# Residual pair with low-rank adapters: half of G early, B0's products and E last, and W0's second identity on GpSimd

## The chip, the cores and the metric

The kernel runs on one core of a Trainium2 chip. Its engines are TensorE (PE in the profile, with its weight loads as PEld), VectorE (DVE), ScalarE (ACT), GpSimd (POOL) and SyncE (SP), which only issues transfers. The metric is the device time of one execution in microseconds. Before the change the median of three runs is 326.9 us (325.46 to 327.69).

## The reference

All is f32. `x` has shape (8, 256, 1024): eight batches of 256 tokens. Two layers with a residual each follow one another, and every batch picks its own adapters by an index:

```python
def layer0(x):   # R = 32, lora_A (5, 1024, 32), lora_B_w (1024, 32)
    base = jnp.einsum('bsi,oi->bso', x, W)
    low = jnp.einsum('bsi,bir->bsr', x, lora_A[labeler_index])
    return base + jnp.einsum('bsr,or->bso', low, lora_B_w) * 0.5

def layer1(x):   # R = 16, lora_As (32, 1024, 16), lora_Bs (32, 16, 1024)
    base_out = jnp.einsum('bti,oi->bto', x, W) + b
    lora_h = jnp.einsum('bti,bir->btr', x, lora_As[adapter_mapping])
    return base_out + jnp.einsum('btr,bro->bto', lora_h, lora_Bs[adapter_mapping]) * 2.0

x = x + layer0(x)
x = x + layer1(x)
```

Written as matrices, one batch is multiplied by (I + W0)ᵀ(I + W1)ᵀ, and small products of rank 32 and 16 are added to it.

## The kernel before

**Algebra.** The kernel first multiplies the two weight matrices, identities added, and afterwards sends all eight batches through that one 1024x1024 product M. Three small products carry the adapters through the weights: G, the eight adapters A of layer 1 times I + W0 (`prepare_down`, two halves h of 512 columns, kept in `gT`); B0, layer 0's shared factor, times I + W1 (`prepare_up`, two halves); and E, the product of B0 and A (`prepare_cross`). Large products are made from 512x512 or 256x256 blocks by a scheme of seven block multiplications in place of eight, so sums of blocks, made by VectorE, are operands of TensorE.

**Storage.** `w0n` holds W0 as eight slices k of 128 rows by 1024 columns. `load_w0(k, i)` (L173, transfer at L176) loads 512 of the columns of one slice. `diag_w0(k)` (L180, operation at L182) adds the identity to a slice: for k below 4 (`NB`) in the first 512 columns, from 4 up in the second. `w1T` holds W1 transposed. It comes as quarters `wq[h, i]` loaded to `units` by `load_w1` (L163, transfers at L168), each of four transfers with runs of 512 bytes, and turned by VectorE in `turn_w1` (L225: transposes at L227, the identity at L235, by VectorE for h = 0 and by GpSimd for h = 1). The first 256 rows of W1's first quarter come another way: as `w1_rows` (L945), turned by TensorE against an identity (L977) and copied out by VectorE and ScalarE (L1022, L1021), with the identity added at L1030.

**Order.** Every engine runs its instructions in the order in which the program writes them (`manual_schedule`). Transfers issued by SP and ScalarE share eight completion semaphores in turn, so a new transfer is issued only when the one that had the semaphore before has landed. SP issues, in this order: `w1_rows`, W0's slices 0 to 3 (first columns), the rest of W1's first quarter, W1's second quarter, W0's slices 4 to 7, B0, W1's third and fourth quarters, then W0's second columns (L1059) and x (L153). The adapters A are loaded by GpSimd (`load_a1`, L193) behind a one-element copy that waits for the first kept product (L195), and repacked by eight copies (L203).

**TensorE.** After a few warming matmuls and the transposes come 32 matmuls of the first product of four row groups (`first`, L1010 and L1012): 16 for the left 256 columns and 16 for the right. `keep_p1` (L294, ScalarE copy at L296) saves them. Two `Second` objects (L609; `one` and `other`) multiply the second product by the seven-part scheme, with `zero_inner` (L644), `z_sums` (L474), `Second.op.sums` (L416) and copies out by `keep` (L503, L505). Then come `prepare_up(0)`, `prepare_down(0)`, `prepare_up(1)`, `prepare_down(1)` and `prepare_cross()`, and then the main products (`mult`, L280, matmul at L282), the first of which is product 6 of `w_groups[0]` and needs the sums `sums_w1_first` (L354: L355 and L356) and `sums` (L260: L268, L269, L274, L275). While these run, VectorE turns the third and fourth quarters, forms M's first rows (`form`, L584, L601 to L607), adds W0's identities of slices 4 to 7 in the midst of `sums_w1_first` (L1072 to L1074), and makes the sums.

Of the kernel before, what the change touches and what calls it, by code (L numbers as in the profile page):

```python
# [10 lines left out]
ALU = mybir.AluOpType  # L11
# [9 lines left out]
P = 128  # L21
# [3 lines left out]
MLOW = 64  # L25
BIAS = 48
NWARM = 6
# [6 lines left out]
NQ = NH // 2  # L34
NB = 4
# [6 lines left out]
def kernel(  # L42
# [51 lines left out]
    ident = const.tile([P, P], F32, tag="ident", name="ident")  # L94
# [9 lines left out]
    m22 = const.tile([P, NB, NH], F32, tag="m22", name="m22")  # L104
# [54 lines left out]
    def new_w1(h: int, i: int):  # L159
        both = units[:, 4 * h + 2 * i : 4 * h + 2 * i + 2].rearrange("p u n -> p (u n)")  # L160
        return both.rearrange("p (t c) -> p t c", t=NR)

    def load_w1(wq, h: int, i: int, lo: int = 0, hi: int = NR):  # L163

        rows = slice(h * NH + lo * SQ, h * NH + hi * SQ)
        for g in range(NG):
            cols = slice(i * NH + g * P, i * NH + (g + 1) * P)
            nc.sync.dma_start(  # L168
                wq[g * SQ : (g + 1) * SQ, lo:hi, :],
                w1[rows, cols].rearrange("(t q) c -> q t c", q=SQ),  # L170
            )

    def load_w0(k: int, i: int):  # L173
        cols = slice(i * NH, (i + 1) * NH)
        rows = w0[(k // NB) * NH : (k // NB + 1) * NH, cols]
        nc.sync.dma_start(  # L176
            w0n[:, k, cols], rows.rearrange("(p m) c -> p m c", m=NB)[:, k % NB, :]
        )

    def diag_w0(k: int):  # L180
        diag = w0n[:, k].rearrange("p (i q m) -> p i m q", i=2, m=NB)[:, k // NB, k % NB]
        nc.vector.tensor_tensor(diag, diag, ident, ALU.add)  # L182

    def load_b0():
        nc.sync.dma_start(
            b0.rearrange("p (i m) r -> p i (m r)", i=2),
            lora_b0.rearrange("(i p m) r -> p i (m r)", i=2, m=NB),
        )
# [2 lines left out]
    a1_rows = work[:, 0 : 2 * NH].rearrange("p (b k r) -> p b k r", b=B, k=NK)  # L191

    def load_a1():  # L193

        nc.gpsimd.tensor_copy(a1_rows[0:1, 0, 0, 0:1], m22[0:1, 0, 0:1])  # L195
        for b in range(B):
            j = index(fixed1, b, N1, mybir.EngineType.Pool)
            nc.gpsimd.dma_start(
                a1_rows[:, b].rearrange("p (i m) r -> p i (m r)", m=NB),
                lora_a1[bass.ds(j, 1)].rearrange("o (i p m) r -> p (o i) (m r)", i=2, m=NB),  # L200
            )
        for b in range(B):
            nc.gpsimd.tensor_copy(a1[:, :, b, :], a1_rows[:, b])  # L203
# [45 lines left out]
    def new_bank():  # L249
        ring.append(ring.pop(0))  # L250
        return ring[-1]
# [382 lines left out]
    def load_inner(ps, tiles):  # L634

        p = m22[:, tiles, :].rearrange("p m (h n) -> p (m h) n", h=2)
        for i, part in ((2, 0), (4, 2), (5, 3)):
            nc.scalar.copy(slot(ps, i), p[:, part])
# [77 lines left out]
    def prepare_up(h: int):  # L716
        pm = new_bank()
        for k in range(NK):
            g = k % 4
            nc.tensor.matmul(  # L720
                pm[g * R0 : (g + 1) * R0, :],
                b0[:, k, :],
                w1T[:, k, h * NH : (h + 1) * NH],
                start=(k < 4),
                stop=(k >= NK - 4),
            )
        nc.scalar.copy(ups[1][:, h * NH : (h + 1) * NH], pm)
# [13 lines left out]

    gT = [work[:, (4 + h) * NH : (5 + h) * NH] for h in range(NO)]

    def prepare_down(h: int):
        pm = new_bank()
        for k in range(NK):
            nc.tensor.matmul(  # L747
                pm,
                a1[:, k].rearrange("p b r -> p (b r)"),
                w0n[:, k, h * NH : (h + 1) * NH],  # L750
                start=(k == 0),
                stop=(k == NK - 1),
            )
        nc.scalar.copy(gT[h], pm)
# [182 lines left out]
    with tc.manual_schedule(engines=ORDERED):  # L937
        make_identity(nc, ident)
        mid = NR // 2
        wq = {}  # L940
# [2 lines left out]
        w1_rows = units[:, 0].rearrange("p (t c) -> p t c", t=2)  # L943
        for t, engine in enumerate((nc.sync, nc.scalar)):
            engine.dma_start(w1_rows[:, t], w1[t * P : (t + 1) * P, 0:NH])  # L945
        for k in range(NB):
            load_w0(k, 0)
        load_w1(wq[0, 0], 0, 0, mid, NR)
        wq[0, 1] = new_w1(0, 1)
        load_w1(wq[0, 1], 0, 1)  # L950
        for k in range(NB, NK):
            load_w0(k, 0)
        load_b0()
        for i in range(2):
            wq[1, i] = new_w1(1, i)
            load_w1(wq[1, i], 1, i)
        nc.scalar.copy(s_all[:, 0:R0], ident[:, 0:R0])


        def warm_up(first, last):  # L960
            for n in range(first, last):
                bank, i = banks[6 + n // 4], n % 4
                nc.tensor.matmul(
                    bank[:, i * P : (i + 1) * P],
                    ident,
                    ident,
                    start=(i == 0),
                    stop=True,
                    skip_group_check=True,
                )  # L970

        warm_up(0, NWARM)
        w1_turned = [banks[4 + t].rearrange("p (m q) -> p m q", m=NB) for t in range(2)]
        for t in range(2):
            for m in range(NB):
                rows = w1_rows[:, t].rearrange("p (q m) -> p m q", m=NB)[:, m]
                nc.tensor.matmul(  # L977
                    w1_turned[t][:, m, :],
                    rows,
                    ident,  # L980
                    start=(m == 0),
                    stop=True,
                    is_transpose=True,
                    skip_group_check=True,
                )
        warm_up(4, 7)
        raw0, raw1 = load_indices(idx0, 0), load_indices(idx1, 1)
        nc.gpsimd.memset(scale, L1_SCALING)
        for half in range(2):
# [20 lines left out]
        def first(g, k: int, n: int):  # L1010
            cols = slice(n * NH // 2, (n + 1) * NH // 2)
            nc.tensor.matmul(  # L1012
                g.p1[:, cols],
                g.a[0][:, k, :],
                w1T[:, k, cols],
                start=False,
                stop=(k == NB - 1),
                skip_group_check=True,
            )

        nc.scalar.copy(w1T[:, 0:NB, P : 2 * P], w1_turned[1])  # L1021
        nc.vector.tensor_copy(w1T[:, 0:NB, 0:P], w1_turned[0])  # L1022
        for k in range(NB):
            diag_w0(k)
            if k == 0:

                part = w1T[0:MLOW, 0, 0:1]
                diag = bass.AP(part.tensor, part.offset, [part.ap[0], [D + 1, NB], [NB, MLOW]])
                same = ident[0:MLOW, 0:MLOW].unsqueeze(1).to_broadcast([MLOW, NB, MLOW])
                nc.vector.tensor_tensor(diag, diag, same, ALU.add)  # L1030
            for g in w_groups:
                first(g, k, 0)
        fixed0, fixed1 = fix_indices(raw0, N0, 0), fix_indices(raw1, N1, 1)
        for k in range(NB):
            turn_w1(wq[0, 0], 0, k, mid, NR)
        seconds = [Second(n) for n in range(2)]
        one, other = seconds
        zero_inner(one.ps)
        for m, g in enumerate(w_groups):
            for k in range(NB):  # L1040
                first(g, k, 1)
            g.keep_p1(m22[:, m, :])
            if m % 2:
                load_inner(seconds[m // 2].ps, seconds[m // 2].tiles)
        load_a1()
        for k in range(NB, NK):
            turn_w1(wq[0, 1], 0, k)
        one.products([1, 2])
# [11 lines left out]
            load_w0(k, 1)  # L1060
        other.products([6, 5, 4, 7, 3])
        keep(other.kept, other.ps)
        prepare_up(0)
        prepare_down(0)
        for k in range(NB):
            turn_w1(wq[1, 0], 1, k)
        one.form()
# [1 line left out]
            turn_w1(wq[1, 1], 1, NB + k)  # L1069
        for k in range(NB):  # L1070
            sums_w1_first(k)
            if k == 1:  # L1072
                for n in range(NB, NK):
                    diag_w0(n)  # L1074
        prepare_up(1)
        prepare_down(1)
        prepare_cross()
        w_groups[0].sums()
        sums_w1_last()
# [280 lines left out]
```

## Time and profile before

| what | value |
|---|---|
| median of three runs | 326.9 us |
| the profiled execution, whole | 325.97 us |
| its span in the profile | 323.9 us |
| granted TensorE clock | full throughout |
| matmul L1012, 32 of 128x256 in two passes | 7.05 to 21.5 us |
| products of `one` and `other` (L527) | 21.49 to 33.9 us |
| `prepare_up(0)`, `prepare_down(0)` | 33.93, 35.78 us |
| `prepare_up(1)`, `prepare_down(1)`, `prepare_cross` | 42.85, 45.38, 52.45 us |
| DMA queue of SP, software queue of GpSimd, whole span | 20.87 MB, 15.01 MB |

Starts are counted from the start of the span. The stretches of the profile below give busy microseconds of each engine with the number of its instructions behind it, then the granted clock, the share of the DMA engines' time, and GB/s.

```profile
core 0: us, PE busy (x) PEld busy (x) DVE busy (x) ACT busy (x) POOL busy (x), PEclk, DMA share, GB/s
0.00:7.00 7.00, 4.84 (x26) 4.54 (x26) 3.61 (x8) 2.09 (x3) 5.15 (x22) 1.00 0.68 230
7.00:21.50 14.50, 14.21 (x65) 12.56 (x66) 9.40 (x23) 2.65 (x6) 2.68 (x5) 1.00 1.18 208
21.50:36.00 14.50, 14.50 (x74) 11.14 (x73) 13.82 (x26) 5.23 (x13) 6.44 (x13) 1.00 1.20 179
36.00:53.00 17.00, 17.00 (x64) 6.61 (x63) 13.55 (x21) 2.12 (x4) 2.46 (x4) 1.00 0.65 172
53.00:115.00 62.00, 62.00 (x212) 39.61 (x208) 56.14 (x102) 14.34 (x30) 24.71 (x28) 1.00 0.70 125
115.00:324.00 209.00, 205.40 (x1062) 172.56 (x1060) 157.20 (x314) 33.43 (x71) 28.63 (x36) 1.00 0.37 89
```

Each f32 matmul of the program appears as two records. The share of DMA time can pass 1[...].

### The profile page before, as it was taken

The numbers are of one execution on the slowest core, as the hardware profiler recorded it, in microseconds if no ns is written. First come the engines' busy times: TensorE is split into PE (matmuls) and PEld (weight loads), VectorE is DVE, ScalarE is ACT, GpSimd is POOL, SyncE is SP. The second block draws the span as 40 slices with busy tenths as digits, with TensorE's granted clock in tenths as the row PEclk, the third lists the DMA queues.
The fourth block names the chain that finished last, engine by engine and source line by source line (L and its number), as shares of the span: only waits on it lengthen the run. The fifth ranks groups of instructions, "written<-read, shape, count | busy, mean of one in ns | idle before, by whom it ended". The sixth has DMA issues, their size and how long they took to land.

```text
span 323.9 us, 4417 instructions
## 1 busy us (share of the span) xinstructions
PE 317.9 (98%) x1494; PEld 247.0 (76%) x1494; DVE 253.7 (78%) x490; ACT 59.9 (18%) x125; POOL 70.1 (22%) x107
## 2 busy tenths in 40 slices
PE   7999999999999999999999999999999999999995
PEld 6888434444588878888878888878888878888884
DVE  5679599879999899999969686929775929632965
ACT  2052215000224223640010420000240000222000
POOL 6053232455132231671004000003100000000000
PEclk9999999999999999999999999999999999999999
DMA  7999954987264995796417610235630111100113
GB/s 223 188 227 171 267 127 78 170 139 152 56 100 85 193 165 95 112 172 108 129 68 187 153 34 0 92 104 146 156 74 0 65 67 65 65 2 0 66 67 130
DMA packets 64910, 36.42 MB, mean 112 GB/s; under 512 B 45508, under 2 KB 58932, under 8 KB 64888
## 3 DMA queue, kind: packets, MB, share of 16 engines
q1 hardware_dynamic: 56088, 20.87, 29.7%
q0 software_dynamic: 8656, 15.01, 22.5%
q8 instruction: 12, 0.20, 0.2%
q10 hardware_dynamic: 144, 0.26, 0.2%
q14 instruction: 10, 0.08, 0.1%
HBM read 19.02 MB, written 8.39 MB: 85 GB/s over the span
## 4 chain that ended last, share of the span: by engine, by line
PE 94%; DMA 3%; DVE 1%; issue 0%; SPq 0%; DVEq 0%
PE bank L527 71%; PE bank L282 11%; PE bank L797 4%; PE bank L747 4%; DMA units<-in_L_cond_W_dram 3%; PE bank L1012 2%; PE bank L720 1%; DVE w1T L227 1%; PE bank L815 1%; DVE w1T L235 0%; PE bank L761 0%; PE bank L547 0%; DVE work L885 0%; SPq L168 0%; DVEq L227 0%
## 5 line engine op out<-in xcount | busy, mean ns | idle before, releaser
L509 DVE TENSOR_TENSOR work<-bank,work 128x512 f32<-128x512 f32 (+1 forms) x56 | 32.1, 618 | 30.6 <-PE bank L527 15.4
L505 ACT COPY work<-bank 128x512 f32<-128x512 f32 (+1 forms) x60 | 27.6, 546 | 77.3 <-PE bank L527 52.2
L931 POOL DMA_DIRECT2D out_dram<-work x12 | 8.9, 743 | 115.8 <-DVE work L607 115.8
L240 DVE STREAM_TRANSPOSE units<-units 128x512 f32<-128x512 f32 x32 | 20.1, 680 | 6.8 <-DMA units<-in_x_dram 6.8
L527 PE MATMUL bank<-w0n,w1T 128*128 128x256 f32 x104 | 24.1, 379 | 0.0
L527 PE MATMUL bank<-w1T,s_all 128*128 128x256 f32 x88 | 22.3, 379 | 0.0
L527 PEld LDWEIGHTS bank<-w0n,w1T 128*128 128x128 f32 x104 | 19.8, 190 | 2.7
L527 PE MATMUL bank<-w0n,m 128*128 128x256 f32 x88 | 20.9, 380 | 0.0
L227 DVE STREAM_TRANSPOSE w1T<-units 128x512 f32<-128x512 f32 (+1 forms) x16 | 14.9, 984 | 6.9 <-DMA w0n<-in_L_cond_W_dram 3.7
L527 PEld LDWEIGHTS bank<-w0n,m 128*128 128x128 f32 x88 | 16.6, 190 | 2.6 <-issue 0.4
L527 PEld LDWEIGHTS bank<-w1T,s_all 128*128 128x128 f32 x88 | 16.7, 190 | 2.3
L527 PE MATMUL bank<-tw,m 128*128 128x256 f32 x68 | 16.8, 379 | 0.0
L527 PE MATMUL bank<-tw,s_all 128*128 128x256 f32 x64 | 16.1, 379 | 0.0
L805 ACT ACTIVATE a<-bank,shift,scale 128x256 f32<-128x256 f32 x4 | 2.3, 564 | 72.4 <-PE bank L797 72.4
L1012 PE MATMUL bank<-w1T,w0n 128*128 128x256 f32 x64 | 14.4, 382 | 0.9 <-DVE w1T L1030 0.7
L527 PE MATMUL bank<-m,units 128*128 128x256 f32 x64 | 15.1, 379 | 0.0
L797 PE MATMUL bank<-units,down 128*64 128x256 f32 x128 | 14.7, 382 | 0.0
L1012 PEld LDWEIGHTS bank<-w1T,w0n 128*128 128x128 f32 x64 | 12.4, 196 | 2.7 <-DVE w1T L1030 0.9
L527 PE MATMUL bank<-w0n,s_all 128*128 128x256 f32 x56 | 14.4, 379 | 0.0
L747 PE MATMUL bank<-w0n,a 128*128 128x512 f32 x32 | 14.3, 599 | 0.0
L527 PEld LDWEIGHTS bank<-tw,m 128*128 128x128 f32 x68 | 12.9, 190 | 1.8
L282 PE MATMUL bank<-tw,s_all 128*128 128x512 f32 x32 | 14.2, 595 | 0.0
(263 smaller groups left out, 662.1 us busy)
## 6 DMA issues: line engine op xcount, KB each, us to landing
units<-in_x_dram SPq DMA_DIRECT2D x128, 64.0 KB, 2.4
out_dram<-work POOLq DMA_DIRECT2D x12, 512.0 KB, 3.5
w0n<-in_L_cond_W_dram SPq DMA_DIRECT2D x16, 256.0 KB, 7.7
units<-in_L_cond_W_dram SPq DMA_DIRECT2D x13, 256.0 KB, 8.7
out_dram<-work SPq DMA_DIRECT2D x3, 512.0 KB, 2.8
down<-in_L_cond_lora_A_dram SPq DMA_DIRECT2D x32, 32.0 KB, 2.6
w1T<-m POOLq DMA_DIRECT2D x4, 256.0 KB, 5.3
s_all<-units POOLq DMA_DIRECT2D x2, 512.0 KB, 5.3
```

The costliest lines, as they stand in the source:

```text
L227: nc.vector.transpose(w1T[:, k, cols].rearrange("p (t q) -> p t q", q=SQ), wq[:, lo:hi].rearrange("p t (q m) -> p m t q", m=NB)[:, k % NB],)
L240: nc.vector.transpose(xT[:, NX * j : NX * (j + 1), :].rearrange("p c (t q) -> p c t q", q=SQ), xq[:, :, j, :].rearrange("p t (q c) -> p c ...
L282: nc.tensor.matmul(pm, a[:, k, :], b(k), start=first and k == 0, stop=(k == NB - 1), skip_group_check=not first,)
L505: nc.scalar.copy(at_home(v, n), whole(ps, n))
L509: nc.vector.tensor_tensor(at_home(v, n), whole(ps, n), at_home(v, n), ALU.add)
L527: nc.tensor.matmul(slot(ps, i) if dst is None else dst, lhs, rhs, start=BANK[i][0] not in started, stop=stop, skip_group_check=True,)
L720: nc.tensor.matmul(pm[g * R0 : (g + 1) * R0, :], b0[:, k, :], w1T[:, k, h * NH : (h + 1) * NH], start=(k < 4), stop=(k >= NK - 4),)
L747: nc.tensor.matmul(pm, a1[:, k].rearrange("p b r -> p (b r)"), w0n[:, k, h * NH : (h + 1) * NH], start=(k == 0), stop=(k == NK - 1),)
L797: nc.tensor.matmul(pl[n * MLOW : (n + 1) * MLOW, :], downs[n][:, k, :], x_b[f"{n + 1}{k // NB + 1}"][:, k % NB, :], start=(k == 0), stop=( ...
L815: nc.tensor.matmul(pl, join, low, start=True, stop=True, skip_group_check=True)
L931: eng.dma_start(out[b, :, h * NH : (h + 1) * NH].rearrange("(j p) d -> p j d", p=P), ob[:, 0:D].rearrange("p (j d) -> p j d", d=NH),)
L1012: nc.tensor.matmul(g.p1[:, cols], g.a[0][:, k, :], w1T[:, k, cols], start=False, stop=(k == NB - 1), skip_group_check=True,)
```

## The change

The change is confined to the first 53 us of the program.

- *Start.* W1's first rows are turned per slice m of four: two transposes into a bank of its own, a copy (VectorE for slice 0, ScalarE for 1 to 3), a 64x64 identity. Slice 3 is turned behind the first four products. Six warming matmuls remain of nine (18 records to 12). Of the four groups, those that don't need W0's identity of slice k are multiplied first.
- *SP's queue.* W0's slices 0 and 1, the rest of W1's first quarter, W0's slices 2 and 3; then, behind a one-element memset of VectorE, W0's slices 4 to 7, and only after them W1's second quarter, B0 and the rest.
- *A.* Six of its eight loads are issued by ScalarE, two by GpSimd, as soon as the indices are fixed. They stand in ScalarE's order ahead of `keep_p1`.
- *The second 16 products of L1012* go by slice for the first two slices of all groups, then by pairs of groups for the last two.
- *G.* Half 0 is multiplied right behind them, ahead of `one` and `other`; half 1 behind `other`; then `prepare_up(0)`, `prepare_up(1)` and `prepare_cross` together.
- *W0's second identity.* GpSimd adds it, ahead of its identities of W1's last quarter (L235) in its own order.

```diff
     def diag_w0(k: int):
...
-        nc.vector.tensor_tensor(diag, diag, ident, ALU.add)
+        engine = nc.vector if k < NB else nc.gpsimd
+        engine.tensor_tensor(diag, diag, ident, ALU.add)
...
     def load_a1():
-
-        nc.gpsimd.tensor_copy(a1_rows[0:1, 0, 0, 0:1], m22[0:1, 0, 0:1])
         for b in range(B):
-            j = index(fixed1, b, N1, mybir.EngineType.Pool)
-            nc.gpsimd.dma_start(
+            engine = nc.scalar if b < 6 else nc.gpsimd
+            j = index(fixed1, b, N1, engine.engine)
+            engine.dma_start(
...
-    def prepare_down(h: int):
-        pm = new_bank()
+    def prepare_down(h: int, pm):
...
-        for k in range(NB):
+        for k in range(2):
             load_w0(k, 0)
         load_w1(wq[0, 0], 0, 0, mid, NR)
-        wq[0, 1] = new_w1(0, 1)
-        load_w1(wq[0, 1], 0, 1)
-        for k in range(NB, NK):
+        for k in range(2, NB):
             load_w0(k, 0)
-        load_b0()
-        for i in range(2):
-            wq[1, i] = new_w1(1, i)
-            load_w1(wq[1, i], 1, i)
...
+        def turn_first(m: int):
+            for t in range(2):
                 nc.tensor.matmul(
+                    banks[4 + m][:, t * P : (t + 1) * P],
+                    w1_rows[:, t].rearrange("p (q m) -> p m q", m=NB)[:, m],
                     ident,
...
+            copy = nc.scalar.copy if m else nc.vector.tensor_copy
+            copy(w1T[:, m, 0:NQ], banks[4 + m][:, 0:NQ])
+
+        def diag_first(m: int):
+            diag = w1T[0:MLOW, m, 0:NQ].rearrange("p (q m) -> p m q", m=NB)[:, m]
+            nc.vector.tensor_tensor(diag, diag, ident[0:MLOW, 0:MLOW], ALU.add)
...
+        for m in range(2):
+            turn_first(m)
+            diag_first(m)
+            if m == 0:
+                diag_w0(0)
         for k in range(NB):
-            diag_w0(k)
...
+            if k + 2 < NB:
+                turn_first(k + 2)
+                diag_first(k + 2)
+            if k:
+                diag_w0(k)
+            if k == 1:
+                fixed1, fixed0 = fix_indices(raw1, N1, 1), fix_indices(raw0, N0, 0)
+
+                nc.vector.memset(w0n[0:1, NB:NK, 0:1], 0.0)
 
-            for g in w_groups:
+            for g in sorted(w_groups, key=lambda g: g.m % 2 == k % 2):
                 first(g, k, 0)
-        fixed0, fixed1 = fix_indices(raw0, N0, 0), fix_indices(raw1, N1, 1)
+        for k in range(NB, NK):
+            load_w0(k, 0)
+        load_a1()
+        wq[0, 1] = new_w1(0, 1)
+        load_w1(wq[0, 1], 0, 1)
+        load_b0()
+        for i in range(2):
+            wq[1, i] = new_w1(1, i)
+            load_w1(wq[1, i], 1, i)
...
-        for m, g in enumerate(w_groups):
-            for k in range(NB):
+        for k in range(NB // 2):
+            for g in w_groups:
                 first(g, k, 1)
-            g.keep_p1(m22[:, m, :])
-            if m % 2:
-                load_inner(seconds[m // 2].ps, seconds[m // 2].tiles)
-        load_a1()
+        for both in (slice(2, 4), slice(0, 2)):
+            for k in range(NB // 2, NB):
+                for g in w_groups[both]:
+                    first(g, k, 1)
+            for g in w_groups[both]:
+                g.keep_p1(m22[:, g.m, :])
+        for s in seconds:
+            load_inner(s.ps, s.tiles)
+        prepare_down(0, banks[3])
...
         keep(other.kept, other.ps)
-        prepare_up(0)
-        prepare_down(0)
+        for n in range(NB, NK):
+            diag_w0(n)
+        prepare_down(1, new_bank())
...
             sums_w1_first(k)
-            if k == 1:
-                for n in range(NB, NK):
-                    diag_w0(n)
+        prepare_up(0)
         prepare_up(1)
-        prepare_down(1)
         prepare_cross()
```

More of the change, by code (lines that the diff above doesn't have):

```diff
@@ L945 @@
             engine.dma_start(w1_rows[:, t], w1[t * P : (t + 1) * P, 0:NH])
-        for k in range(NB):
+        for k in range(2):
             load_w0(k, 0)
         load_w1(wq[0, 0], 0, 0, mid, NR)
-        wq[0, 1] = new_w1(0, 1)
-        load_w1(wq[0, 1], 0, 1)
-        for k in range(NB, NK):
+        for k in range(2, NB):
             load_w0(k, 0)
-        load_b0()
-        for i in range(2):
-            wq[1, i] = new_w1(1, i)
-            load_w1(wq[1, i], 1, i)
         nc.scalar.copy(s_all[:, 0:R0], ident[:, 0:R0])
-        def warm_up(first, last):
-            for n in range(first, last):
-                bank, i = banks[6 + n // 4], n % 4
+        for n in range(NWARM):
+            bank, i = banks[4 + n // 2], n % 2
+            nc.tensor.matmul(
+                bank[:, NQ + i * P : NQ + (i + 1) * P],
+                ident,
+                ident,
+                start=(i == 0),
+                stop=True,
+                skip_group_check=True,
+            )
+        def turn_first(m: int):
+            for t in range(2):
                 nc.tensor.matmul(
-                    bank[:, i * P : (i + 1) * P],
+                    banks[4 + m][:, t * P : (t + 1) * P],
+                    w1_rows[:, t].rearrange("p (q m) -> p m q", m=NB)[:, m],
                     ident,
[L966 to L981, printed above, removed]
+                    start=(m >= NWARM // 2 and t == 0),
                     stop=True,
@@ L985 @@
                 )
-        warm_up(4, 7)
+            copy = nc.scalar.copy if m else nc.vector.tensor_copy
[3 more added lines that the diff above has]
+            nc.vector.tensor_tensor(diag, diag, ident[0:MLOW, 0:MLOW], ALU.add)
         raw0, raw1 = load_indices(idx0, 0), load_indices(idx1, 1)
@@ L1019, in first @@
             )
-        nc.scalar.copy(w1T[:, 0:NB, P : 2 * P], w1_turned[1])
-        nc.vector.tensor_copy(w1T[:, 0:NB, 0:P], w1_turned[0])
-        for k in range(NB):
-            diag_w0(k)
[L1025 to L1030, printed above, removed]
-            for g in w_groups:
-                first(g, k, 0)
-        fixed0, fixed1 = fix_indices(raw0, N0, 0), fix_indices(raw1, N1, 1)
+        for m in range(2):
[3 more added lines that the diff above has]
+                diag_w0(0)
+        fixed0 = fixed1 = None
+        for k in range(NB):
+            if k + 2 < NB:
[7 more added lines that the diff above has]
+            for g in sorted(w_groups, key=lambda g: g.m % 2 == k % 2):
+                first(g, k, 0)
+        for k in range(NB, NK):
[7 more added lines that the diff above has]
+            load_w1(wq[1, i], 1, i)
         for k in range(NB):
```

## The prediction

> **What bounds the kernel now.** I read the page's engine shares first, then the chain of work that ended last, then TensorE's waits over the whole span, then the timeline of the first 54 us engine by engine.
>
> ```profile
> PE 317.9 (98%) x1494; PEld 247.0 (76%) x1494; DVE 253.7 (78%) x490; ACT 59.9 (18%) x125; POOL 70.1 (22%) x107
> ...
> PE bank L963 <- POOL ident masks.py:199: 1.5, 1, 1.5
> PE bank L1012 <- DVE w1T L1030: 0.7, 1, 0.7
> PE bank L1012 <- DVE w1T L235: 0.2, 1, 0.2
> ```
>
> TensorE waits three times, 2.4 us in all, and never after 15.77. In the chain in order of time it runs from there to 320.4. So whatever lets it enter that run earlier shortens the kernel by that much, and any new wait in the run lengthens it one for one. Nothing that only frees another engine counts. The lines that decide are these, of the timeline:
>
> ```profile
> 7.05 8.08 PEld L1012 LDWEIGHTS bank<-w1T,w0n 128*128 128x128 f32 x38 [0.89 <-DVE w1T L1030]
> ...
> 18.09 4.13 DVE L227 STREAM_TRANSPOSE w1T<-units 128x512 f32<-128x512 f32 x4 [1.77 <-DMA units<-in_L_cond_W_dram]
> ...
> 28.91 4.11 DVE L227 STREAM_TRANSPOSE w1T<-units 128x512 f32<-128x512 f32 x4
> ...
> 39.28 4.11 DVE L227 STREAM_TRANSPOSE w1T<-units 128x512 f32<-128x512 f32 x4 [3.73 <-DMA w0n<-in_L_cond_W_dram]
> ...
> 40.47 0.53 POOL L235 TENSOR_TENSOR w1T<-w1T,ident 128x128 f32<-128x128 f32 x1 [5.20 <-DVE w1T L227]
> ...
> 43.33 0.64 DVE L355 TENSOR_TENSOR tw<-w1T 128x512 f32<-128x512 f32 x1
> ...
> 46.15 1.26 DVE L182 TENSOR_TENSOR w0n<-w0n,ident 128x128 f32<-128x128 f32 x4
> ...
> 50.69 0.69 DVE L269 TENSOR_TENSOR s_all<-s_all,w0n 128x512 f32<-128x512 f32 x1
> ...
> 53.02 7.13 PE L282 MATMUL bank<-tw,s_all 128*128 128x512 f32 x16
> ```
>
> The reader is to see the last part. The first main product (L282, product 6 of group 0) needs sum 269 of VectorE, done at 51.38. TensorE comes to it at 53.02, so VectorE leads by 1.64 us. VectorE's only hole is the 3.73 us before the transposes of the last quarter of W1, whose last load landed at 39.1 (issued 24.2, 14.9 to landing). The DMA engines are full from 4 to about 40 us. One more number matters, of the issues of L176 in the window 39 to 39.5: the last slice of W0's second columns is issued at 39.1 and lands 6.7 us later, at **45.8**.
>
> **The change, part by part.** Everything is reckoned as the start of L282, 53.0 now, for three limits: TensorE's own work, VectorE's chain, GpSimd's queue. The latest decides.
>
> *Start.* Before, eight transposes and two 128x512 copies (0.69 and 0.59) go ahead of the 64x256 diagonal (0.65), and the first product starts at 7.05. After, two transposes do: rows land at 4.26, done 4.96; a 128x256 copy of VectorE, some 0.4 by the half of 0.69 plus overhead; a 64x64 diagonal, 0.27 by L235. First product at about 5.8, 1.25 earlier. VectorE then gets diagonal 3 (it waits for the transpose behind the first four products and ScalarE's copy, to about 8.5) ahead of W0's slice 1 (0.4), so products of slice 1 wait some 0.5 at 8.7. Two transposes between products cost 0.22, restarts 0.25. The 64 records of 0.216 (13.8) then end at 20.6, against 21.5 now: **0.9 earlier**. The new order of the second half removes the 0.24 wait; that is in the 20.6.
>
> *TensorE's work from there.* Before, 53.0 - 21.5 = 31.5 us, with a wait of 0.38 for bank zeroing and about 0.7 of L720 behind GpSimd's diagonals (2.61 against 1.92 for the first one). Without them 30.5. The five prepared products only change places: TensorE alone would reach L282 at 20.6 + 30.5 = **51.1**, 1.9 earlier. This is the whole gain to be had.
>
> *A's loads (`load_a1`).* G's half 0 now runs at 20.6, not 35.8. Its eight loads go from GpSimd at 18.4 to ScalarE (six) and GpSimd (two) at about 10.5, after the indices (9.75). ScalarE issues two of them only when an earlier W0 slice has landed (14 to 15); its copies L296 behind them are first needed near 18.5, so that is hidden. GpSimd's two took 8.3 to 10.8 to land: 19 to 21, plus a copy of 0.3 each. Cost 0 (cover: the second half of the products) to 1; I take 0.3, inside later slack.
>
> *SP's queue.* W0's slices 4 to 7 move ahead of W1's second quarter and, by the small memset, behind VectorE at about 10.2. By 9.4 the engines have moved 2 MB, which is all that is issued by then, so they run dry. Before, SP went on issuing from 5.3. From the first issue (0.90) to the first bytes took 1.1, so the lull is about 1.9. Of the 0.5 MB of A (the eight adapters of layer 1, `a`) in smaller packets I assume the same time as now. The last loads come from the engine that lags most, which has less of a lull: I take 0.7, ends 0 and 1.9. W1's second quarter needs the 4.5 MB that were in at 21.4 before (the landing of W0's slice 7), plus the lull, plus A's at some 2.3: **24.4**, against 18.0.
>
> *VectorE's chain.* From that landing to L269's end: 28.91 - 18.09 = 10.8; transposes 4.1; forming 2.6 (32.92 to 35.55); transposes 4.1; eight sums 5.45 (43.33 to 49.97, less the 1.26); two sums 1.4; in all 28.5. So 24.4 + 28.5 = **52.9**. Before, 18.0 + 28.5 + 3.7 of hole + 1.3 of L182 = 51.5, as seen. Moving G's product ahead has eaten the hole. On the way TensorE may stand 0.5 to 1 at the second products (bank zeroing L646 comes at 24.4 + 5.6, TensorE at 29.4); this is beside the later limit.
>
> *The second identity by GpSimd.* It takes 1.26 off VectorE, as four operations of some 0.53 (L235, the same shape). The row says VectorE's transposes took 4.11 beside L235 and 4.11 without it, but one sum (L356) took 0.90 beside it instead of 0.69. The Trainium skill, "Perfetto Trace Analysis", section "Optimizing Scalar/DVE Operations", says that GpSimd and VectorE share an SBUF read port, so that moving work between them might not help. By the rule, if every GpSimd operation blocked VectorE, 4 x 0.53 = 2.1 would come back and the step would cost 0.85 net, VectorE's chain being 55.0. By the row, beside transposes nothing comes back and 1.26 stays saved. I take the row, with 0.2 for one sum.
>
> What the step does to GpSimd's own queue is worse. In program order the four stand **ahead of L235**, the diagonals of W1's last quarter, and each waits for its slice of W0, the last at 45.8. VectorE's sums L355 wait for L235. So: last slice, +0.1, identity 0.53, +0.1, first L235 0.53, +0.05, then 6.85 to the end of L269 (5.45 + 1.4): landing + 8.15. With an unchanged landing, 45.8 + 8.15 = 53.95. With 0.7 of lull, 46.5 less 0.2 for A's loads that no longer fall between W1's: 46.3, so **54.45**. Ends: 43.0 (the slow engine catches up in the lull and A no longer goes through GpSimd's descriptors) gives 51.15; 48.5 (full lull, and x's loads squeezed in as now) gives 56.65. Meanwhile TensorE runs G's other half, waiting slice by slice, until about 47.8, then B0's two products and E, 4.5, and stands about 2 us at L282.
>
> *Others at nothing.* ACT's later copies, the loads of x and of A0 behind SP (x is turned from 98.8, A0 multiplied from 115.2) and the rearranged banks stay under the 35 us of L282. After L282 VectorE has lost its lead of 1.64, but 60 to 70 us shows it busy 6.51 of 10, so it gets this back.
>
> **Sum.** Start of L282 at 54.4 against 53.0: +1.4. Span 323.9 + 1.4 = 325.3; with the 2.07 around the span of the profiled execution (325.97) 327.4. The median shown, 326.9, is 0.9 above that execution, so **328.3**.
>
> **The rivals.**
> 1. *As meant.* The last slice lands by 43 and W1's quarter by 22.5; TensorE sets the pace: 51.1 to 51.7, 325.0 to 325.6. For it: A's loads ride in free time, and the slowest engine may use the lull. Against it: the same bytes must still pass a queue full until 40. 17%.
> 2. *VectorE's chain sets it* at 52.5 to 53.3: the slice is early but W1's quarter is late, 326.4 to 327.2. The change moves waits and gives nothing. 18%.
> 3. *The slower side: SP pinned behind the memset.* The DMA lull costs its full 1.9 or more and the last W0 slice lands after 48.2; there 8.15 more passes 56.35, 3.3 behind. At 49 the time is 331.0. For it: SP issued nothing less than full before. Against it: one engine lags the others by some us, so not all the lull is lost. 14%.
> Forecast (326.9 + 0.3 to 3.2: 327.2 to 330.1): 51%.
>
> **Numbers.** 1% is 3.3 us, about what a measurement of this kernel can tell from no change: 323.6 to 330.2. Faster than that isn't reached by rival 1 even whole (1.9 of gain); I leave 0.03 for an estimate of mine that is wrong. Slower: rival 3, 0.14, and a tail of the forecast, 0.15. Within: 0.82. The range leaves out the lower half of rival 1 and the upper half of rival 3: 325.3 to 330.7. The likeliest case alone is 327.2 to 330.1.
>
> **What would show it.** Right: TensorE waits for VectorE's sum L269 ahead of L282 for about 2 us; GpSimd's identities of W0 end with the last slice's landing, and L235 follows; L355 waits for GpSimd; first product near 5.8; hole in the DMA row at 10 to 11. Wrong: L282 starts before 52 with no wait (rival 1); the wait is there but L235 was done long before, with VectorE busy throughout (rival 2); A's copies end after 21.5 and TensorE stands ahead of G's half, which I hold to be hidden.

## The result, and the profile after

| | median, us | executions | ratio to before |
|---|---|---|---|
| before | 325.31 (324.3 to 327.69) | 22 | |
| after | 326.05 (325.02 to 328.03) | 22 | 1.003, 95% interval 1.0017 to 1.0044 |

The change costs about 1.0 us by this ratio (0.3% of 325.3; 0.55 to 1.4 by the interval); the means differ by 0.93, the medians by 0.74. The first three runs of the kernel before, of which the prediction took its level, lay high: their median 326.9 is 1.6 above that of all 22. The profiled execution of after took 327.88 us, its span 326.2; it is one of the longer ones, and the text below says where it is not typical.

TensorE's waits over the whole span of after (time in all, number, longest):

```profile
PE bank L282 <- DVE s_all L269: 2.0, 1, 2.0
PE bank L956 <- POOL ident masks.py:199: 1.5, 1, 1.5
PE bank L746 <- POOL a L203: 0.3, 1, 0.3
PE bank L967 <- DMA units<-in_L_cond_W_dram: 0.2, 1, 0.2
```

There is now a wait of 2.0 us ahead of the first main product. It was not there before. The timeline of after, with the lines that answer to those of before (line numbers have moved by a few; L1008 was L1012, L746 was L747):

```profile
6.22 3.78 PE L1008 MATMUL bank<-w1T,w0n 128*128 128x256 f32 x8
...
10.22 12.76 PE L1008 MATMUL bank<-w1T,w0n 128*128 128x256 f32 x56
...
23.27 7.13 PE L746 MATMUL bank<-w0n,a 128*128 128x512 f32 x16 [0.28 <-POOL a L203]
...
26.60 4.04 DVE L227 STREAM_TRANSPOSE w1T<-units 128x512 f32<-128x512 f32 x4 [9.29 <-DMA units<-in_L_cond_W_dram]
...
44.28 4.08 DVE L227 STREAM_TRANSPOSE w1T<-units 128x512 f32<-128x512 f32 x4
...
45.69 0.53 POOL L183 TENSOR_TENSOR w0n<-w0n,ident 128x128 f32<-128x128 f32 x1 [0.56 <-DMA w0n<-in_L_cond_W_dram]
46.16 1.01 POOL L235 TENSOR_TENSOR w1T<-w1T,ident 128x128 f32<-128x128 f32 x2
...
48.29 0.64 DVE L355 TENSOR_TENSOR tw<-w1T 128x512 f32<-128x512 f32 x1
...
54.48 0.69 DVE L269 TENSOR_TENSOR s_all<-s_all,w0n 128x512 f32<-128x512 f32 x1
...
55.32 1.95 PE L282 MATMUL bank<-tw,s_all 128*128 128x512 f32 x4 [1.96 <-DVE s_all L269]
```

VectorE's hole has moved. Before, there were 1.77 us ahead of W1's second quarter and 3.73 ahead of the last; now there are 9.29 ahead of the second quarter, and from 26.60 to the end of L269 at 55.17 VectorE works without a stop. GpSimd does let W1's identity (L235) stand behind the last slice of W0, but the first of them is done at 46.7, before VectorE has turned the quarter (48.36).

The DMA lull is where it was forecast. Stretches of before and then of after (busy time by engine, granted clock, share of DMA time, GB/s):

```profile
9.50:12.00 2.50, 2.50 (x13) 2.26 (x13) 1.11 (x8) 0.00 (x0) 0.00 (x0) 1.00 1.24 194
```

```profile
9.50:12.00 2.50, 2.50 (x10) 1.83 (x9) 1.02 (x7) 0.37 (x1) 0.00 (x0) 1.00 0.24 86
```

One thing in the timeline nobody asked for: the first eight records of L1008 take 3.78 us, 0.43 apart, where before they came 0.216 apart. In this execution TensorE ran at half speed until 10.8 us; the first record of the full clock is there, at 4.9 in the trace of before. (The clock's column says 1.00 in both rows above because it has no record earlier than that; the full clock given for the kernel before holds from 4.9 on.)

### The profile page after: what moved, and what is told of

It reads as the page before. It is cut to its first block, busy times and chain, and to the rows that moved or that the text cites. A ratio compares the mean times of both kernels' runs of the same rounds, so it can differ in the third digit from the quotient of the medians.

```text
span 326.2 us, 4400 instructions
## 1 busy us (share of the span) xinstructions
PE 318.7 (98%) x1488; PEld 248.3 (76%) x1488; DVE 252.2 (77%) x490; ACT 60.1 (18%) x127; POOL 67.0 (21%) x104
## 4 chain that ended last, share of the span: by engine, by line
PE 84%; DMA 10%; SPq 4%; DVE 1%; issue 0%; ACT 0%; ACTq 0%; DVEq 0%
PE bank L527 66%; PE bank L282 11%; DMA units<-in_L_cond_W_dram 6%; PE bank L796 4%; SPq L168 2%; DMA w0n<-in_L_cond_W_dram 2%; SPq L153 1%; PE bank L1008 1%; DMA work<-in_L_cond_lora_As_dram 1%; DMA down<-in_L_cond_lora_A_dram 1%; PE bank L967 1%; PE bank L814 1%; DVE s_all L269 0%; DVE s_all L268 0%; SPq L138 0%
## 5 line engine op out<-in xcount | busy, mean ns | idle before, releaser
L1008 PE MATMUL bank<-w1T,w0n 128*128 128x256 f32 x64 | 16.5, 420 | 0.0
L282 PE MATMUL bank<-tw,s_all 128*128 128x512 f32 x32 | 14.1, 594 | 2.0 <-DVE s_all L269 2.0
L1008 PEld LDWEIGHTS bank<-w1T,w0n 128*128 128x128 f32 x64 | 13.7, 219 | 2.4 <-DVE w1T L981 0.4
L746 PE MATMUL bank<-w0n,a 128*128 128x512 f32 x32 | 14.2, 595 | 0.3 <-POOL a L203 0.3
```

Of the source, the lines that this page charges most:

```text
L282: nc.tensor.matmul(pm, a[:, k, :], b(k), start=first and k == 0, stop=(k == NB - 1), skip_group_check=not first,)
L746: nc.tensor.matmul(pm, a1[:, k].rearrange("p b r -> p (b r)"), w0n[:, k, h * NH : (h + 1) * NH], start=(k == 0), stop=(k == NK - 1),)
L1008: nc.tensor.matmul(g.p1[:, cols], g.a[0][:, k, :], w1T[:, k, cols], start=False, stop=(k == NB - 1), skip_group_check=True,)
```

## The experiments

Three theories were tried. **G**, the prediction's: GpSimd's queue sets L282. **V**: VectorE's own chain from the landing of W1's second quarter does. **C**: the clock of TensorE turns a small wait into a larger loss.

### Eight warming matmuls (e1_warm8)

```diff
-NWARM = 6
+NWARM = 8
```

> The changed kernel with eight warming matmuls in place of six, so that TensorE stays busy until W1's first rows land. Theory C (clock): in the changed kernel's trace the full clock comes at 10.8 us instead of 4.9, because a short wait for the rows breaks the busy stretch; the longer warm-up brings it back to about 5 in nearly all executions: the group of executions near 327.4 thins out (9 of 22 now), median 325.3 to 325.6, ratio to before about 1.000 to 1.001. Rival (no clock effect, the two groups come from elsewhere): median stays 326.0 and the upper group stays at 4 of 10.

326.24 us, ratio 1.004 (1.0019 to 1.006): no gain. The profile has the full clock from 5.6, but the two extra matmuls run ahead of the transposes at half speed, the first product starts at 6.61, and L282 comes at 53.57 behind a wait of 2.2 us. Six of 22 executions had a mean granted clock of 0.995, at 327.8 to 329.2. A late start does not show in that mean (the execution traced for after has 0.998), so these six lost their clock later; where they did was not traced. The value of this run is as a trace of the changed order with an early clock.

### Before with six warming matmuls of nine (e2_before_short)

```diff
-        warm_up(4, 7)
```

> The kernel before with six warming matmuls in place of nine (the three behind the transposes left out). Theory C: TensorE then has nothing from 5.7 to 7.05 and more executions raise the clock late, so a second group some 2 us higher appears more often than before's 3 of 22, the ratio is 1.002 to 1.004. Rival: the three matmuls do nothing, ratio 1.000 and the groups as before.

325.69 us, ratio 1.0014 (0.9992 to 1.0036), inconclusive as a ratio; but five of 22 executions lie at 328.3 to 328.5, where the kernel before on the same chip had none of 51 above 327.6. The profile, of another execution (326.97), caught the clock's rise at 11.1 us, and its L282 came at 54.04, 1.0 later than in the profile of before. What makes the five longer by some 3 us was not traced. That leaving out the three matmuls makes a late clock more frequent is not shown: e12_before_ident below has all nine of them, and four of its 20 executions lie at 327.6 to 328.4. The changed kernel dropped the same three.

### GpSimd's two identities exchanged (e3_pool_order)

```diff
+            turn_w1(wq[1, 1], 1, NB + k)   # moved up: L235 now ahead
         for n in range(NB, NK):
             diag_w0(n)
         prepare_down(1, new_bank())
-            turn_w1(wq[1, 1], 1, NB + k)
```

> e1_warm8 with GpSimd's two kinds of identities in the other order: first W1's last quarter (L235), then W0's (L183); TensorE's order is unchanged. Theory G (the prediction's: L355 waits for L235, which waits behind the last slice of W0): L282 starts 1 to 1.5 us earlier than in e1_warm8, time 1 us less. Theory V (VectorE's own chain from the landing of W1's second quarter sets L282): no change, within 0.2 us of e1_warm8; TensorE may even lose 0.5 to 1 ahead of G's second half, since W0's identities come later.

329.64 us, ratio 1.0124 (1.0098 to 1.0151). L235 ran directly behind the transposes (first done at 43.5) and L269 still ended only at 53.72, against 53.42 in e1_warm8. This alone would not settle it, for the sums start 0.75 earlier here than there and then lose that beside W0's identities. The trace of e1_warm8 does:

```profile
40.13 0.90 DVE L604 TENSOR_TENSOR units<-units 128x512 f32<-128x512 f32 x1
...
43.72 0.52 POOL L235 TENSOR_TENSOR w1T<-w1T,ident 128x128 f32<-128x128 f32 x1 [0.49 <-DVE w1T L227]
...
46.52 0.66 DVE L355 TENSOR_TENSOR tw<-w1T 128x512 f32<-128x512 f32 x1
```

GpSimd, with W0's identities behind it, waits there for VectorE's transposes, and VectorE never for GpSimd. **Theory G falls.** In e3_pool_order TensorE instead waited for W0's identities, 3.7 us from 44.05. Timeline of this run, VectorE and GpSimd side by side, and then its stretches:

```profile
40.15 0.69 DVE L604 TENSOR_TENSOR units<-units 128x512 f32<-128x512 f32 x1
...
45.77 0.67 DVE L355 TENSOR_TENSOR tw<-w1T 128x512 f32<-128x512 f32 x1
...
46.77 3.73 POOL L183 TENSOR_TENSOR w0n<-w0n,ident 128x128 f32<-128x128 f32 x4
47.28 1.00 DVE L355 TENSOR_TENSOR tw<-w1T 128x512 f32<-128x512 f32 x1
```

```profile
40.00:47.30 7.30, 4.05 (x11) 1.71 (x9) 7.20 (x11) 1.84 (x4) 2.93 (x5) 1.00 0.59 135
47.30:50.70 3.40, 2.91 (x4) 1.35 (x5) 3.33 (x5) 0.00 (x0) 3.20 (x4) 0.50 0.31 61
50.70:54.00 3.30, 3.30 (x18) 1.10 (x20) 3.23 (x6) 0.59 (x1) 0.00 (x0) 1.00 0.20 32
```

Two more readings. The identity takes 0.93 (3.73 / 4) beside VectorE's sums, and a sum 1.00 in place of 0.67; in the changed kernel, beside forming and transposes, it took 0.55. And the second row shows the granted clock at 0.50: it fell 3.3 us into the wait, and stayed down for 3.4 us, 2.9 of them with TensorE back at work (from 47.79).

### Without the memset (e4_no_memset)

```diff
-                nc.vector.memset(w0n[0:1, NB:NK, 0:1], 0.0)
```

(on e1_warm8)

> e1_warm8 without the one-element memset, so that W0's slices 4 to 7 are issued as soon as a semaphore is free. Theory V: the lull of the DMA engines at 10 to 12 us goes, W1's second quarter lands 1.5 to 2 us earlier, VectorE's chain and L282 move by as much as TensorE allows: 1 to 1.5 us less than e1_warm8, below before by 0.3 to 1. Theory G: the last slice of W0 lands 0.7 earlier and so does L282. Rival: W0's slices 2 and 3 are slowed by the new traffic and TensorE waits for them at 8 to 10 us; no gain.

325.55 us, ratio 1.0001 (0.9984 to 1.0018); e1_warm8 stood at 1.004. The lull is gone (DMA share 1.06 from 9.5 to 12), W1's second quarter is turned from 22.1 instead of 24.7, the wait at L282 falls from 2.2 to 1.2, and none of 14 executions is at 0.995. The gain on e1_warm8, about 1.3 by the ratios, is of the size that theory V expected; the time did not fall below before. The landing came 2.5 earlier and L269 only 0.7 (52.74), since VectorE now stands 1.5 us ahead of its forming step, waiting for ScalarE's copies of the second product. As the run also brings W0's last slice earlier, it does not part V from G.

### Sixteen idle matmuls ahead of L282 (e5_fill)

```diff
         prepare_cross()
+        for n in range(16):
+            nc.tensor.matmul(
+                banks[7][:, P : 2 * P], ident, ident, start=True, stop=True, skip_group_check=True
+            )
```

> The changed kernel with 16 idle matmuls of the identity (some 1.8 us, into an unused part of a bank) between E and L282, where TensorE waits 2.0 us. Theory C2: in about a third of the executions that wait itself makes the clock fall to half for one stretch of 3.4 us, as it did in the trace of e3_pool_order; those are the executions with a mean clock of 0.995 (6 of 22 of the changed kernel, 327.0 to 328.0). The filler leaves no wait over 0.5, the executions at 0.995 go, and the median falls by 0.3 to 0.6 to about 325.6. Rival: the 0.995 has another cause, and its share stays, or the filler pushes L282 back and the time rises by up to 0.5.

328.15 us, ratio 1.0094 (1.0067 to 1.0121): a miss of mine. An idle matmul costs 0.23, not 0.11, since each makes two records, and the filler ran from 51.39 to 55.06, past the end of L269 at 52.51. As a trace it helps: it is the changed kernel with the clock early (its rise is at 5.1), and its sums are ready at 52.5, not at 55.2.

### W0's second identity back on VectorE (e6_ident_dve)

```diff
-        engine = nc.vector if k < NB else nc.gpsimd
-        engine.tensor_tensor(diag, diag, ident, ALU.add)
+        nc.vector.tensor_tensor(diag, diag, ident, ALU.add)
...
         one.form()
+        for n in range(NB, NK):
+            diag_w0(n)
+        prepare_down(1, new_bank())
```

> The changed kernel with W0's second identity back on VectorE, just ahead of the transposes of W1's last quarter. Theory V: VectorE's chain sets L282, so its four operations (1.26) come on top, more if they wait for the last slice of W0; L282 1.3 to 3 us later, time 1.3 to 3 more than the changed kernel, and more executions at 0.995 for the longer wait. Theory G: GpSimd's queue is free again, L235 directly behind the transposes, so 0.5 to 1.5 less.

329.06 us, ratio 1.01 (1.0072 to 1.0127), 3 more than the changed kernel: theory V again, and against G. L282 came at 53.67, behind a wait of 2.4 us (e5_fill's sums would have let it start near 52.7). That is about 1 us, under the 1.3 to 3 expected of the step; VectorE's chain itself grew by 0.7, from 28.5 (e5_fill) to 29.2. The rest is put down to the clock: 9 of 12 executions have a mean of 0.995 or less. The trace of one of them shows the wait (in this run L282 is line 281, and L269 line 268) and the fall at the place:

```profile
PE bank L281 <- DVE s_all L268: 2.4, 1, 2.4
```

```profile
50.00:53.90 3.90, 1.48 (x25) 0.74 (x18) 3.80 (x7) 2.32 (x5) 1.11 (x2) 1.00 0.22 36
53.90:57.30 3.40, 3.40 (x5) 1.39 (x5) 3.40 (x7) 1.34 (x3) 1.40 (x2) 0.51 1.04 151
57.30:60.00 2.70, 2.70 (x7) 1.14 (x6) 2.70 (x6) 0.60 (x2) 2.46 (x3) 0.99 0.79 146
```

TensorE is back at work at 53.67, and from 53.9 to 57.3 it works all the time at half clock: 1.7 us lost after the wait is over.

### No memset, and B0's load last (e7_no_memset_b0)

```diff
-                nc.vector.memset(w0n[0:1, NB:NK, 0:1], 0.0)
...
-        load_b0()
         for i in range(2):
             wq[1, i] = new_w1(1, i)
             load_w1(wq[1, i], 1, i)
+        load_b0()
```

> The changed kernel without the memset, and with B0's load behind W1's last quarter. Theory V with the last loads: without the lull W1's last quarter lands about 41 and, B0 (128 KB) being behind it, at about 41; L282 near 52, wait under 0.7, no executions at 0.995; 325.0 to 325.4, at or below before. Rival: TensorE's late clock at the start, still there in some executions, keeps the median at 325.5 or more.

325.22 us, ratio 0.9993 (0.9976 to 1.0009): level with before. The wait at L282 is 0.8; one of 22 executions is at 0.995. VectorE stands 1.6 us ahead of its forming step, as it did in e4_no_memset, so the last load no longer sets its chain.

### All of A's loads by GpSimd (e8_a_pool)

```diff
-            engine = nc.scalar if b < 6 else nc.gpsimd
+            engine = nc.gpsimd
```

> The changed kernel with all of A's loads issued by GpSimd. They no longer take turns with SP's loads on the eight shared semaphores, so W1's second quarter is issued and lands 1 to 2 us earlier (Theory V: L282 1 us earlier) if the semaphores held it back. But A lands later: the eighth issue comes 7 us behind the first, at about 19, and needs 5 or more to land, so TensorE waits ahead of G's first half by 2 to 4 us, which costs as much as it is not absorbed by the wait at L282: 0 to 2 slower than the changed kernel. If the semaphores are no matter, W1's second quarter lands as now.

332.56 us, ratio 1.0221 (1.0189 to 1.0253). TensorE waits 6.9 us for A ahead of G's first half (20.71 to 27.62), more than I had reckoned, and the clock falls 5.2 us into the wait, for 6.8 us. W1's second quarter is turned from 24.4, about as in e5_fill (24.0): there is no sign that the shared semaphores hold it back.

### Six idle matmuls (e9_fill6)

```diff
+        for n in range(6):
+            nc.tensor.matmul(
+                banks[7][:, P : 2 * P], ident, ident, start=True, stop=True, skip_group_check=True
+            )
         prepare_cross()
```

> The changed kernel with six idle matmuls of the identity ahead of E: e5_fill showed that one costs 0.22, so 1.3 us, less than the wait at L282 (1.8 to 2.0). Theory C2: the executions with a mean clock of 0.995 (6 of 22 of the changed kernel) go, for the wait left is 0.5 to 0.7; median 325.5 to 325.8, 0.3 to 0.5 below the changed kernel's 326.05. Rival: the 0.995 stays at a quarter, median 326.0 or above.

325.27 us, ratio 1.0001 (0.9987 to 1.0015), and none of 14 executions at 0.995. Idle work inside the wait, which can do nothing but keep TensorE busy, takes away the loss: **theory C holds for the wait at L282**. TensorE's waits in the profile (of one of the longest executions, 326.51):

```profile
PE bank L746 <- POOL a L203: 1.1, 1, 1.1
PE bank L282 <- DVE s_all L269: 0.2, 1, 0.2
```

### G's first half back behind the second product (e11_g_late)

```diff
-        prepare_down(0, banks[3])
...
+        prepare_down(0, new_bank())
         prepare_down(1, new_bank())
```

> The changed kernel with G's first half back behind the second product, all else as changed. Theory V: TensorE ends L1012 near 20.8 and W1's second quarter, now behind W0's slices 4 to 7 and A, lands at 24 to 26.5 and is turned by 28 to 30.5, so TensorE waits some 5 to 7 us for it, VectorE's chain stays as it is and L282 goes to about 58: 4 to 6 us slower than the changed kernel, with the clock falling on top. That would show that G's first half pays for its own loads only, by covering them. Rival: W1's second quarter lands earlier without G's early use of the engines, no more than 2 slower.

330.69 us, ratio 1.0151 (1.0118 to 1.0184). TensorE waits 5.2 us ahead of the second product (from 21.50), and the clock falls 3.3 us into the wait, for 6.8 us; L282 comes at 59.42 with no wait. In the new order of loads G's first half is needed as a cover.

### The identity alone, in the kernel before (e12_before_ident)

```diff
-        nc.vector.tensor_tensor(diag, diag, ident, ALU.add)
+        engine = nc.vector if k < NB else nc.gpsimd
+        engine.tensor_tensor(diag, diag, ident, ALU.add)
```

> The kernel before with W0's second identity by GpSimd alone (at its old place, behind L235). TensorE came to L282 1.64 us behind VectorE there, so 1.26 taken from VectorE brings nothing: ratio 0.999 to 1.001. If VectorE's later work mattered it would be below 0.998; if GpSimd's operations slow VectorE's sums by the shared port, VectorE's lead shrinks but the time stays.

325.49 us, ratio 1.0019 (0.9999 to 1.0038): no gain, as expected, though a little above the expected 0.999 to 1.001. Four of 20 executions lie at 327.6 to 328.4, at full mean clock; they were not traced. The four identities took 3.77 us in a row beside the sums.

### Two sums moved ahead (e10_sums_early)

```diff
         one.form()
+        w_groups[0].sums_first()
         for k in range(NB):
             turn_w1(wq[1, 1], 1, NB + k)
...
-        w_groups[0].sums()
+        w_groups[0].sums_last()
```

(on e7_no_memset_b0)

> e7_no_memset_b0 with the first two sums of W0's blocks (L268 and L269, 1.4 us) ahead of the transposes of W1's last quarter, in the hole of 2 us where VectorE waits for its load. Theory V: VectorE's chain after that load shortens by 1.4, starts at most 0.6 later, L282 comes some 0.8 earlier and the wait of 0.78 goes: 324.5 to 324.8, faster than before by 0.2%. Rival: TensorE is late by itself (late clock at the start, A's copies), time as e7_no_memset_b0, 325.2.

**324.07 us, ratio 0.9969 (0.9951 to 0.9986): faster than both kernels**, by 1.0 us against before. Its timeline, VectorE and then TensorE:

```profile
40.66 1.01 DVE L268 TENSOR_TENSOR s_all<-w0n 128x512 f32<-128x512 f32 x1
41.70 0.69 DVE L269 TENSOR_TENSOR s_all<-s_all,w0n 128x512 f32<-128x512 f32 x1
42.31 4.06 DVE L227 STREAM_TRANSPOSE w1T<-units 128x512 f32<-128x512 f32 x4
...
46.98 0.91 DVE L356 TENSOR_TENSOR tw<-tw,w1T 128x512 f32<-128x512 f32 x1
...
51.18 0.69 DVE L356 TENSOR_TENSOR tw<-tw,w1T 128x512 f32<-128x512 f32 x1
```

```profile
50.24 0.62 PE L760 MATMUL bank<-a,b 128*32 128x128 f32 x16
50.79 1.55 PE L282 MATMUL bank<-tw,s_all 128*128 128x512 f32 x3
```

The gain is larger than expected, for another reason than the hole I had named. VectorE did not sit idle there; the sums stand in its way like any other work. But L282's four matmuls need the sums of W0 whole and W1's sums one after the other: with L269 early, the first matmul needs only the first L356 (47.9), and the last L356 is done at 51.87, while the fourth matmul's turn comes 2.6 us after 50.79. TensorE has no wait left there, and L282 starts at 50.8, 0.3 from the 51.1 that the prediction gave for TensorE alone.

## Why the prediction was right and where it was wrong

**Right.** The direction and the kind of loss: a gain at the start, and a new wait of some 2 us at L282 for VectorE's sum L269. The first product was put at 5.8 and came at 5.9 to 6.0 in the traces of e5_fill and e9_fill6. G's first half was put at 20.6 and came at 20.8 in e5_fill, 0.7 before the point that before had reached at 21.5; with the late clock of after the gain at the start is lost. TensorE's own work from there was put at 30.5 and took 30.0 in e10_sums_early (the 0.38 that the prediction took out as a wait is idle time of the weight load, PEld). The lull lies where it was said. W1's second quarter was put at 24.4; it is turned from 24.0 (e5_fill), 24.7 (e1_warm8) and 24.9 (e9_fill6). VectorE's chain from there was put at 28.5 us and measured 28.6 (26.60 to 55.17). A's loads, held to be hidden, made TensorE wait 0.3 us in after and 1.1 in e9_fill6, inside the slack at L282.

**Wrong: the step that named the limit.** The prediction said that GpSimd's queue was the latest of three, "landing + 8.15", with the last slice of W0 at 46.3 and L282 at 54.45. In the traces of e1_warm8, e5_fill and e9_fill6 that slice lands at 42.3 to 43.1, 3 to 4 us before the estimate and at the low end that the prediction gave (43.0); with 8.15 on top, GpSimd's queue would let L269 end at 50.5 to 51.3. Even in the trace of after (45.7) L235 was done ahead of VectorE's need. The limit was rival 2's, VectorE's chain, put at 52.9 and found at 52.5 to 53.8 for an early clock. The error was to take the landing of 45.8 over from before and add a lull: in these three traces SP issued the slice at 36.3 to 37.0, where before had 39.1, and it then took about 6 us to land, where before took 6.7. The engine that lags is there in the trace of before (the trace keeps the landing of each of a transfer's 16 parts: of that slice the last lands 2.2 us behind the fifteenth) and hardly in these (0.5 at most). What let SP issue earlier is not shown.

**Wrong: the sum has no term for the clock.** The prediction let a new wait lengthen the kernel "one for one". With the limit where it was, L282 moved little: the changed kernel with an early clock has its sums ready at 52.5 to 53.8, where L282 stood at 53.0 in the profile of before. With the wait filled (e9_fill6) the ratio is 1.0001, so the loss hangs on the wait, and in part on what the clock makes of it. The table has the wait at L282 in each profile (for e3_pool_order that at G's second half, for e8_a_pool at its first, for e11_g_late at the second product), and the executions whose mean clock was 0.995 or less. That mean is what one stretch of 3.4 us at half clock makes of some 325 us. Such a stretch was traced in e3_pool_order and at L282 in e6_ident_dve; for the other kernels' executions at 0.995 the place is inferred.

| kernel | wait, us | executions at 0.995 or below |
|---|---|---|
| before, beside the experiments | 0 | 0 of 133 |
| e10_sums_early | 0 | 1 of 20 |
| e9_fill6 | 0.2 | 0 of 14 |
| e7_no_memset_b0 | 0.8 | 1 of 22 |
| e4_no_memset | 1.2 | 0 of 14 |
| after | 2.0 | 6 of 22 |
| e1_warm8 | 2.2 | 6 of 22 |
| e6_ident_dve | 2.4 | 9 of 12 |
| e3_pool_order | 3.7 | 6 of 6 |
| e11_g_late | 5.2 | 5 of 5 |
| e8_a_pool | 6.9 | 6 of 6 |

A stretch of 3.4 us at half clock costs 1.7 us if TensorE works through it; six of 22 would give 0.46 in the mean. As measured, those six of after (327.4 in the mean; the other sixteen 326.0) make 0.4 of the 0.93. The other half is not located: in e1_warm8 and e9_fill6 L282 comes at 53.6 and 53.9, up to 0.9 later than before, and three more executions of after lie at 327.3 to 327.9. That the forecast's +1.4 lies near the measured +1.0 is luck: a limit that was not the limit, and no clock.

**Wrong in level.** 328.3 stood on a median of three runs that was 1.6 too high.

**Left open.** The trace of after itself is of another kind: half clock at the start until 10.8, 2 us late from there on. How many of the changed kernel's executions are of this kind is not known (the three at 327.3 to 327.9 have a mean clock of 0.998 or 1.0, and one of them is the traced one), nor is its cause. The single executions at 0.995 of kernels with little or no wait were not traced.

**The rule on the shared port.** The prediction weighed the warning of the Trainium skill ("Perfetto Trace Analysis", section "Optimizing Scalar/DVE Operations") against GpSimd beside VectorE, and took the row of the trace. For transposes the row held: four took 4.08 beside identities and 4.04 without (44.28 and 26.60 in after). For sums both sides were slowed, as the rule warns: 0.93 for an identity, 1.00 for a sum (e3_pool_order). And in the changed kernel the identities fall not only on the last transposes but on forming, which is made of sums: the five forming steps take 3.0 to 3.3 us in after, e1_warm8, e5_fill and e9_fill6, and 2.5 in e3_pool_order and e6_ident_dve, where no identity of GpSimd runs beside them. So 0.5 to 0.8 of the 1.26 that VectorE was freed of came back, where the prediction had put 0.2, and 2.1 for the rule taken whole.

## What to carry to other kernels

When a product is moved ahead to cover late loads, follow the engine that prepares the operands behind those loads: its hole, not its busy share, says how much delay it can take. Price a new wait of a busy TensorE with the clock in it: here, by their mean clock, about a quarter of the executions paid some 1.5 us on top of a wait of two, and cheap idle matmuls, or operands made in the order in which the first product eats them, took the loss away. Take the level from many runs before forecasting an effect of 0.3%.

## What the runs showed of the hardware

The Trainium skill, "TensorE: Matmul & The Clock Gate", section "Why this matters for your kernels", wants no idle gap above some 3 us between bursts of matmuls. Here shorter gaps were enough: in the trace of e6_ident_dve a wait of 2.4 us, in a kernel otherwise hardly idle, was followed by half clock for 3.4 us. By the mean clock the same happened in 9 of its 12 executions, in 12 of 44 with a wait of 2.0 to 2.2 us, and in 2 of 70 with one of 1.2 us or less. The measurement decides. In the longer waits the clock fell before the wait was over, for 3.4 us (e3_pool_order) and for 6.8 us (e8_a_pool, e11_g_late). The section "What's actually happening" of the same page has the clock follow a free-running window of 3.4 us. The steps seen, 3.4 and twice that, fit with it, and so do executions of one kernel that differ; no run here shows the window itself.
